# A second-level seven-product step for the fourth product of a gate-and-up block, with kept parts and right operands in DRAM

## The chip, the cores and the metric

One core of a Trainium2 chip runs the whole program. The metric is the device time of one execution in microseconds (us). The kernel before takes 1083.45 us (median of three runs, 1083.03 to 1083.62).

## The reference

The input `x` has 2 batches of 2048 rows of 512 numbers, all float32. First comes attention over channels (the scores are 512 by 512 for each batch) with a layer norm ahead of it and a residual, then a gated feed-forward block with its own layer norm and residual. The weights of the feed-forward block are given as indices into a table of 16 numbers:

```python
def _ghost_linear(x, idx, lut):
    w = lut[idx]
    return jnp.einsum('bsh,oh->bso', x, w)
gate = _ghost_linear(x, gate_idx, lut)     # idx: (1376, 512)
up = _ghost_linear(x, up_idx, lut)         # idx: (1376, 512)
h = jax.nn.silu(gate) * up
return _ghost_linear(h, down_idx, lut)     # idx: (512, 1376)

x = x + _L0_attn_ref(_layernorm(x, axis=-1), Wq, Wk, Wv, Wo)
x = x + _L0_ffn_ref(_layernorm(x, axis=-1), lut, gate_idx, up_idx, down_idx)
```

The change is in the part that computes `gate` and `up`.

## The kernel before

**Stages.** By the profile's times: the Gram matrices and the small attention products come first, then (up to 286 us) the attention output `y`, then gate and up (286 to 806 us), then the down product (to the end). The order of the instructions on TensorE, ScalarE, VectorE and SyncE is the order in which the program's text makes them (a manual schedule); GpSimd's DMAs are in text order too.

**Units of gate and up.** The 1376 hidden channels are cut into 11 blocks `f` of 128 (the last has 96), the 4096 rows into 4 pairs `p` of two 512-row halves. A unit `(f, p)` is one 2-by-2 block product: the left operand has gate weights in its upper row (A11, A12) and up weights in its lower row (A21, A22); the right operand is the normalised input (`xs[p]`). The four blocks of the result are gate and up, each for two row halves. A unit does it by seven products in place of eight (Strassen's scheme in Winograd's form), with left sums S1 to S4 and right sums T1 to T4. Each product contracts 256 channels: two matmuls of 128x128 by 128x512 in float32, and each of those is two instructions in the profile.

**Steps of a unit**, as `Line.run` writes them: `a1` (A11·B11 into PSUM bank `a`, copied by ScalarE to `p1`), `c1` (S3·T3 into bank `c`, copied to `p7`), `extra1`, then `a4` of the unit before (S4·B22 onto its bank `a`, Silu by ScalarE), `a2` (S2·T2 onto `a`, copied to `u2`), `extra2`, `c2` (A22·T4 onto `c`, added to `u2` by VectorE), `end` of the unit before, `b` (A12·B21, then Silu of the gate half `h0`), `a3` (S1·T1 onto `a`, VectorE makes `c22` from it), `first` (`h0` times `u2`, stored to DRAM). Between the steps `between()` writes pieces of other VectorE work, chiefly the look-ups of weights (`pump`, `Job.ops`: 19 VectorE operations for each of 33 blocks of indices). Four of the products (`a1`, `a2`, `a3`, `a4`) are added up in bank `a`, and what stands there is copied out in between: a step that adds onto a bank can't begin before that copy is done.

```python
u.a2()
self.between()
u.extra2()
u.c2()
if last is not None:
    last.end()
self.between()
one, two = (u.a3, u.b) if final else (u.b, u.a3)
```

**Two levels for one product.** For the blocks `f` from 2 to 9 the product A12·B21 is itself done by seven products for eight over a group of four units: two blocks `f`, `f+1` and two row pairs `p`, `p+1`. The unit's `role` is its place in the group: 0 is (even f, even p), 1 is (even f, odd p), 2 is (odd f, even p), 3 is (odd f, odd p). Role 0 does two single matmuls in `b`, role 1 three (`extra1`, `extra2`, `b`), role 2 two (`extra1`, `b`), role 3 none. What roles 2 and 3 need of role 1 and 2 is kept in SBUF (`r6`, `r5`) and added onto `p1` by an accumulating DMA from GpSimd's queue (L938, L973).

**PSUM.** Eight banks: `a`, `b` and `c` with two buffers each, `x` and `y` with one.

**Look-ups.** `jobs` is the order of the blocks of indices. A job waits (its gate) until buffers are free. The indices are fetched by GpSimd's queue two jobs ahead and converted by ScalarE (`cast`).

Of the kernel before, what the change touches and what calls it, by code (L numbers as in the profile page):

```python
# [58 lines left out]
P = 128  # L60
# [6 lines left out]
def tile_attn_ffn(  # L67
# [228 lines left out]
    l2a, l2b = {}, {}  # L296
    whole = set()
# [3 lines left out]
    def gate_job(f):  # L301
        f0, rows = FT[f]
        n = KB * rows

        def load(queue, idx):
            queue.dma_start(idx, gate_idx[:, KB * f0 : KB * f0 + n])

        def dest():
            t = wgu.tile([P, KB, P], F32, tag="wg", name=f"wg_{f}", bufs=3)
            gw[f] = t.rearrange("p k r -> p (k r)")[:, :n]  # L310
            return gw[f]

        def after():
            gw[f] = gw[f].rearrange("p (k r) -> p k r", k=KB)
            whole.add(f)
            yield 0.1

        return Job(f"g{f}", P, n, load, dest, after, lambda: f < 3 + passed[0])

    def up_job(f):  # L320
        f0, rows = FT[f]
        n = KB * rows
        up = []

        def load(queue, idx):
            queue.dma_start(idx, up_idx[:, KB * f0 : KB * f0 + n])

        def dest():
            t = wgu.tile([P, KB, P], F32, tag="wu", name=f"wu_{f}", bufs=2)
            up.append(t.rearrange("p k r -> p (k r)")[:, :n])  # L330
            return up[0]

        def after():
            g, u = gw[f], up[0].rearrange("p (k r) -> p k r", k=KB)
            t = wgu.tile([P, 3, 2, P], F32, tag="s", name=f"s_{f}", bufs=2)
            a11, a12, a21, a22 = g[:, 0:2, :], g[:, 2:4, :], u[:, 0:2, :], u[:, 2:4, :]
            s1, s2, s4 = (t[:, q, :, :rows] for q in range(3))
            for op, d, v, w in (
                (add, s1, a21, a22), (sub, s2, s1, a11), (sub, a21, a11, a21), (sub, s4, a12, s2)
            ):  # L340
                op(d, v, w)
                yield 0.42
            gu[f] = {"11": a11, "12": a12, "S3": a21, "22": a22, "S1": s1, "S2": s2, "S4": s4}
        return Job(f"u{f}", P, n, load, dest, after, lambda: f < 2 + ended[0])
# [10 lines left out]
    jobs += [down_job(i) for i in range(6)]  # L355
    for f in range(2, NFT - 1, 2):
        jobs += [gate_job(f), up_job(f), gate_job(f + 1), up_job(f + 1), down_job(5 + f // 2)]
# [19 lines left out]

    def pump(us):

        owed[0] = min(owed[0] + us, 2 * us + 1.0)  # L380
        while owed[0] > 0:
            cost = next(lookup, None)
            if cost is None:
                return
            owed[0] -= cost
# [474 lines left out]
    def psum(tag, name):  # L860
        return fps.tile([P, E], F32, tag=tag, name=name, bufs=1 if tag in "xy" else 2)

    def l2_sums(g):

        x11, x21 = xb[4 * g][:, 2, :], xb[4 * g][:, 3, :]
        x12, x22 = xb[4 * g + 2][:, 2, :], xb[4 * g + 2][:, 3, :]
        t = x2p.tile([P, 3, CH], F32, tag=f"l{g}", name=f"l2b_{g}")
        t1, t2, t4 = (t[:, q, :] for q in range(3))
        l2b[g] = {"11": x11, "21": x21, "22": x22, "T1": t1, "T2": t2, "T3": x12, "T4": t4}
        return [  # L870
            lambda: sub(t1, x12, x11), lambda: sub(t2, x22, t1),
            lambda: sub(x12, x22, x12), lambda: sub(t4, x21, t2),
        ]

    def l2_left(f):


        t = wgu.tile([P, 4, P], F32, tag="l", name=f"l_{f}", bufs=1)
        if f == NFT - 1:
            a12 = gu[f]["12"]  # L880
            both, minus = (t[:, q, : FT[f][1]] for q in range(2))
            gu[f]["both"], gu[f]["minus"] = both, minus
            return [
                lambda: add(both, a12[:, 0, :], a12[:, 1, :]),
                lambda: nc.vector.tensor_scalar_mul(minus, a12[:, 0, :], -1.0),
            ]
        a11, a12 = gw[f][:, 2, :], gw[f][:, 3, :]
        a21, a22 = gw[f + 1][:, 2, :], gw[f + 1][:, 3, :]
        s1, s2, s3, s4 = (t[:, q, :] for q in range(4))
        l2a[f // 2] = {"22": a22, "S1": s1, "S2": s2, "S3": s3, "S4": s4}  # L890
        return [
            lambda: add(s1, a21, a22), lambda: sub(s2, s1, a11),
            lambda: sub(s3, a11, a21), lambda: sub(s4, a12, s2),
        ]
# [8 lines left out]

    two = {}

    class GateUp:
# [8 lines left out]
        def pairs(self, a, b):  # L915
            return [(gu[self.f][a][:, kk, :], xs[self.p][b][:, kk, :]) for kk in range(2)]
# [11 lines left out]
        def a1(self):  # L928
            self.a = self.view("a")
            mm(self.a, self.pairs("11", "11"), True)  # L930
            if self.role in (None, 0):
                self.p1 = self.view("b")
            else:
                self.p1 = self.temp("p1")
            nc.scalar.copy(self.p1, self.a)
            if self.role in (2, 3):
                r = two["r6" if self.role == 2 else "r5", self.p // 2]
                nc.gpsimd.dma_start(self.p1, r, accum_op=ALU.add)  # L938

        def c1(self):  # L940
            self.c = self.view("c")
            mm(self.c, self.pairs("S3", "T3"), True)
            self.p7 = self.temp("p7")
            nc.scalar.copy(self.p7, self.c)  # L944

# [5 lines left out]
        def c2(self):  # L951
            mm(self.c, self.pairs("22", "T4"), False)
            add(self.u2, self.c, self.u2)

        def pair(self, a, b):
            return [(l2a[self.f // 2][a], l2b[self.p // 2][b])]

        def kept(self, tag):
            return x2p.tile([P, CH], F32, tag=f"{tag}{self.p // 2}", name=f"{tag}_{self.name}")

        def extra1(self):
            if self.role == 1:
                mm(two["x"], self.pair("S2", "T2"), False)
                two["r6", self.p // 2] = r6 = self.kept("r6")
                nc.scalar.copy(r6, two["x"])
            elif self.role == 2:
                two["y"] = self.view("y")
                mm(two["y"], self.pair("S3", "T3"), True)  # L970
                r7 = x2p.tile([P, CH], F32, tag="r7", name=f"r7_{self.name}")
                nc.scalar.copy(r7, two["y"])
                nc.gpsimd.dma_start(two["r5", self.p // 2], r7, accum_op=ALU.add)  # L973

        def extra2(self):
            if self.role == 1:
                mm(two["x"], self.pair("S1", "T1"), False)
                two["r5", self.p // 2] = r5 = self.kept("r5")
                nc.scalar.copy(r5, two["x"])

        def b(self):
            self.h0 = h0 = self.temp("h0", 2)
            g = self.p // 2
            if self.role is None:
                if self.f == NFT - 1 and self.p % 2:
                    x22, t3 = l2b[g]["22"], l2b[g]["T3"]
                    w = gu[self.f]
                    mm(self.p1, [(w["both"], x22), (w["minus"], t3)], False)
                else:
                    mm(self.p1, self.pairs("12", "21"), False)  # L990
            elif self.role == 0:
                two["x"] = self.view("x")
                mm(two["x"], [(gw[self.f][:, 2, :], l2b[g]["11"])], True)
                mm(self.p1, [(gw[self.f][:, 3, :], l2b[g]["21"])], False)
                nc.scalar.copy(h0, two["x"])
                add(h0, self.p1, h0)
            elif self.role == 1:
                mm(two["x"], self.pair("S4", "22"), False)
                add(h0, two["x"], self.p1)
            elif self.role == 2:  # L1000
                mm(two["y"], self.pair("22", "T4"), False)
                add(h0, two["y"], self.p1)
# [7 lines left out]
        def first(self):  # L1010
            nc.vector.tensor_tensor(self.h0, self.h0, self.u2, ALU.mult)
            self.store(self.h0, 2 * self.p)

        def a4(self):
# [3 lines left out]
            self.h1 = self.temp("h1", 2)  # L1018
# [6 lines left out]
    class Line:  # L1025
# [5 lines left out]
        def run(self, u, final=False):  # L1031
            u.a1()
            self.between()
            u.c1()
# [24 lines left out]

    sums_of = []  # L1060
    todo = []

    def between():
# [3 lines left out]
        elif sums_of and (sums_of[0] | 1) in whole:  # L1067
            for op in l2_left(sums_of.pop()):
                op()
        else:  # L1070
            pump(1.0)
# [81 lines left out]
    class Down:  # L1153
# [95 lines left out]
        extra1 = extra2 = first  # L1249
# [15 lines left out]
    for f, p in units:  # L1265
        while f not in gu or 1 < f < NFT - 1 and p and (f | 1) not in whole:
            next(lookup)
# [3 lines left out]
        elif sums_of:  # L1271
            for op in l2_left(sums_of.pop()):
                op()
        if f == NFT - 1 and p == 0:
# [9 lines left out]
            todo += by_two(l2_left(f) + down_sums(hps["dT"]))  # L1284
# [5 lines left out]
        line.run(GateUp(f, p), final=(f, p) == (NFT - 1, NPR - 1))  # L1290
# [5 lines left out]
        if f == 1 and p % 2:  # L1296
            todo += l2_sums(p // 2)
# [84 lines left out]
```

## Time and profile before

| | |
|---|---|
| time, median of three runs | 1083.45 us |
| time of the profiled execution | 1082.97 us |
| its span, first to last instruction | 1081.2 us |
| TensorE busy | 1075.6 us (99%), clock 1.000 |
| VectorE busy | 742.4 us (69%) |
| ScalarE busy | 340.1 us (31%) |
| GpSimd busy | 57.7 us (5%) |
| VectorE busy from 450 to 500 us | 40.98 us of 50 |
| DMA share from 450 to 500 us | 0.27 |

Matmuls are pipelined: a group of four instructions is shown as 1.88 us long, but the next group starts 1.72 us after it. "Idle before" is the time for which an engine had nothing to do before an instruction, with what released it. PEld is the load of the weights ahead of a matmul.

### The profile page before, as it was taken

What the parts mean: (1) busy time and instruction counts of PE and PEld (TensorE: products, weight loads), DVE (VectorE), ACT (ScalarE), POOL (GpSimd) and SP (SyncE); (2) the same over time, 40 slices, a digit from 0 to 9 for tenths busy, and PEclk for the clock granted to TensorE, in tenths of its full rate; (3) what the DMA queues carried; (4) which work ended last, traced back from release to release, by engine and by line L of the source; (5) the groups of instructions that cost most, each with busy time, mean ns of one, the idle gap of its engine ahead of it and who ended that gap; (6) DMA issues with size and microseconds to landing.
All of it is one profiled execution on the core that took longest, in us unless ns stands there. A gap on an engine that the chain in (4) does not pass through costs nothing.

```text
span 1081.2 us, 10377 instructions
## 1 busy us (share of the span) xinstructions
PE 1075.6 (99%) x3442; PEld 644.9 (60%) x3442; DVE 742.4 (69%) x1610; ACT 340.1 (31%) x631; POOL 57.7 (5%) x94
## 2 busy tenths in 40 slices
PE   9999999999999999999999999999999999999998
PEld 5668886444444444444444444444348888888887
DVE  7888777899888778888787887876643334433341
ACT  4652522555632233323332332333221111111110
POOL 0000000012110000100110020010000000000000
PEclk9999999999999999999999999999999999999999
DMA  8750314597661111331231142123425545345421
GB/s 342 232 166 17 81 40 97 139 231 205 169 163 49 49 50 67 98 84 53 78 97 64 54 109 76 54 74 80 149 58 168 179 155 163 93 141 183 154 68 39
DMA packets 91061, 123.44 MB, mean 114 GB/s; under 512 B 14576, under 2 KB 50672, under 8 KB 90112
## 3 DMA queue, kind: packets, MB, share of 16 engines
q1 hardware_dynamic: 62496, 83.39, 24.4%
q0 software_dynamic: 8448, 22.62, 9.4%
q10 hardware_dynamic: 20064, 16.78, 4.9%
q8 instruction: 27, 0.44, 0.2%
q14 instruction: 26, 0.21, 0.1%
HBM read 68.76 MB, written 47.71 MB: 108 GB/s over the span
## 4 chain that ended last, share of the span: by engine, by line
PE 93%; DVE 4%; ACT 2%; issue 1%; ACTq 0%; DMA 0%; DVEq 0%
PE a_g L899 28%; PE a_d L899 14%; PE c_g L899 14%; PE y L754 8%; PE c_d L899 7%; PE gp L438 4%; PE b_d L899 4%; PE b_g L899 3%; PE x_g L899 3%; PE ea_t L591 1%; PE ea_p L591 1%; PE ea_m L591 1%; PE y_g L899 1%; PE ea_s L591 1%; PE ec_p L591 1%; PE ec_m L591 1%
## 5 line engine op out<-in xcount | busy, mean ns | idle before, releaser
L754 PE MATMUL y<-m,nT 128*128 128x512 f32 x256 | 110.4, 592 | 0.0
L135 DVE TENSOR_TENSOR u<-c_g,u 128x512 f32<-128x512 f32 (+1 forms) x44 | 30.4, 691 | 102.0 <-PE c_g L899 102.0
L754 PEld LDWEIGHTS y<-m,nT 128*128 128x128 f32 x256 | 48.5, 190 | 60.7 <-issue 57.3
L899 PE MATMUL a_g<-xb,wg 128*128 128x512 f32 (+1 forms) x176 | 82.7, 592 | 0.0
L899 PE MATMUL c_g<-xb,wu 128*128 128x512 f32 (+1 forms) x176 | 82.7, 592 | 0.0
L899 PE MATMUL a_g<-xb,s 128*128 128x512 f32 (+1 forms) x176 | 82.7, 592 | 0.0
L899 PE MATMUL a_g<-xT_a,s 128*128 128x512 f32 (+1 forms) x176 | 82.7, 592 | 0.0
L438 PE MATMUL gp<-xn_a 128*128 128x128 f32 (+3 forms) x256 | 70.1, 434 | 0.4 <-ACT xn_a L231 0.3
L899 PE MATMUL a_g<-xT_sq,s 128*128 128x512 f32 (+1 forms) x132 | 62.0, 592 | 0.0
L438 PEld LDWEIGHTS gp<-xn_a 128*128 128x128 f32 x256 | 43.9, 190 | 27.7 <-issue 15.1
L899 PEld LDWEIGHTS a_g<-xb,s 128*128 128x128 f32 (+1 forms) x176 | 33.0, 188 | 42.6 <-issue 38.2
L899 PEld LDWEIGHTS a_g<-xT_a,s 128*128 128x128 f32 (+1 forms) x176 | 33.0, 188 | 42.5 <-issue 42.5
L899 PEld LDWEIGHTS c_g<-xb,wu 128*128 128x128 f32 (+1 forms) x176 | 33.0, 188 | 42.5 <-issue 42.5
L899 PEld LDWEIGHTS a_g<-xb,wg 128*128 128x128 f32 (+1 forms) x176 | 33.0, 188 | 42.5 <-issue 42.3
L289 DVE COPY_PREDICATED wd<-b_wd,wd 128x512 f32<-128x512 int16 (+1 forms) x77 | 56.4, 733 | 1.6
L899 PE MATMUL a_d<-dT,hs_a 128*128 128x256 f32 x224 | 56.2, 378 | 0.0
L135 DVE TENSOR_TENSOR r<-r,a_d 128x256 f32<-128x256 f32 x32 | 13.5, 421 | 53.4 <-PE a_d L899 53.4
L899 PEld LDWEIGHTS a_d<-dT,hs_a 128*128 128x128 f32 x224 | 42.4, 189 | 6.0
L277 DVE TENSOR_SCALAR wd<-idx_wd,lut_x,lut_sb 128x512 int32<-128x512 int32 (+1 forms) x88 | 44.5, 538 | 0.0
L899 PEld LDWEIGHTS a_g<-xT_sq,s 128*128 128x128 f32 (+1 forms) x132 | 24.8, 188 | 31.9 <-issue 31.3
L899 PE MATMUL c_g<-xT_a,wu 128*128 128x512 f32 (+1 forms) x88 | 41.5, 593 | 0.2 <-ACT p L944 0.2
L944 ACT COPY p<-c_g 128x512 f32<-128x512 f32 (+1 forms) x44 | 25.8, 585 | 48.2 <-PE c_g L899 43.5
(285 smaller groups left out, 1926.2 us busy)
## 6 DMA issues: line engine op xcount, KB each, us to landing
hd<-h SPq DMA_DIRECT2D x80, 256.0 KB, 2.0
h<-hd SPq DMA_DIRECT2D x40, 512.0 KB, 6.3
nl<-nd SPq DMA_DIRECT2D x32, 256.0 KB, 5.6
xnd<-xn_f ACTq DMA_DIRECT2D x16, 512.0 KB, 5.5
fl<-xnd POOLq DMA_DIRECT2D x32, 256.0 KB, 6.5
xn_back<-xnd SPq DMA_DIRECT2D x32, 256.0 KB, 3.5
out_dram<-r SPq DMA_DIRECT2D x31, 256.0 KB, 2.9
x<-in_x_dram SPq DMA_DIRECT2D x7, 1024.0 KB, 13.8
```

The costliest lines, as they stand in the source:

```text
L135: nc.vector.tensor_tensor(dest, a, b, ALU.add)
L277: vec.tensor_scalar(dest.bitcast(I32), idx, lut_x[:rows, k : k + 1], lut_i[:rows, at : at + 1], ALU.bitwise_and, ALU.bitwise_xor,)
L289: vec.copy_predicated(dest, masks[level - 1], t)
L438: nc.tensor.matmul(gp[b][i][:, i * P :], xn[:, i, j % 2, :], xn[:, i:, j % 2, :], start=c % CPB == 0 and j == 0, stop=c % CPB == CPB - 1 a ...
L591: nc.tensor.matmul(ps[:, m, :], self.a[a][:, k, m * P : (m + 1) * P], self.b[b][:, k, :], start=first and m == k == 0, stop=k == 1, skip_g ...
L754: nc.tensor.matmul(ys[k], nTs[k][:, i, :], m[:, i, :], start=(i == 0), stop=(i == KB - 1))
L899: nc.tensor.matmul(ps, lhsT, rhs, start=first and i == 0, stop=i == len(pairs) - 1, skip_group_check=not first,)
L944: nc.scalar.copy(self.p7, self.c)
```

## The change

The product A22·T4 (in `c2`) is now done over the same groups of four units by seven products for eight, as A12·B21 is. The bank `y` is gone and a bank `z` stands in its place: `x` serves A12·B21 in all roles, `z` serves A22·T4. Role 0 does two single matmuls in `c2` (one of them into `z`); role 1 three (a new step `extra0`, `extra1`, `c2`); role 2 two (`extra0`, `c2`); role 3 none. `c2` of role 3 issues nothing. The right operands' sums and the kept parts of both products go to DRAM and are loaded again or added from there: the kept parts are added by GpSimd's accumulating DMAs onto `p1` as before and, for the new product, onto a new copy `v` of bank `c`. `uw` keeps the looked-up weights of up; their sums (`of_both`) are put off, so that up's look-ups run one block ahead (three buffers of `wu` for two). `h0` and `h1` have one buffer for two. The order of the jobs and the rate of `pump` change.

```diff
-        return fps.tile([P, E], F32, tag=tag, name=name, bufs=1 if tag in "xy" else 2)
+        return fps.tile([P, E], F32, tag=tag, name=name, bufs=1 if tag in "xz" else 2)
...
+    class Second:
...
+            def made(tag, u, v):
+                r[tag] = x2p.tile([P, CH], F32, tag="rt", name=f"{tag}_{self.name}{g}", bufs=3)
+                sub(r[tag], u(), v())
+                far = self.far[g, tag] = dram.tile(
...
+                nc.sync.dma_start(far, r[tag])
...
+        def load(self, g, *tags):
+            for tag in tags:
+                t = x2p.tile([P, CH], F32, tag="tt", name=f"{tag}_{self.name}{g}_in", bufs=7)
+                nc.sync.dma_start(t, self.far[g, tag])
+                self.right[g][tag] = t
...
+        def part(self, u, tag, onto=False):
...
+            t = x2p.tile([P, CH], F32, tag="rt", name=f"{tag}_{self.name}_{u.name}", bufs=3)
+            nc.scalar.copy(t, self.ps)
+            if onto:
+                nc.gpsimd.dma_start(self.parts[g, tag], t, accum_op=ALU.add)
+                return
...
+            nc.sync.dma_start(to, t)
+
+        def add_part(self, u, dest):
+            tag = {2: "r6", 3: "r5"}.get(u.role)
+            if tag:
+                nc.gpsimd.dma_start(dest, self.parts[u.p // 2, tag], accum_op=ALU.add)
...
+    of_b = Second("b", "x", lambda f: in_two(gw[f][:, 2:4, :]), lambda p: in_two(xs[p]["21"]))
+    of_c = Second("c", "z", lambda f: in_two(uw[f][:, 2:4, :]), lambda p: in_two(xs[p]["T4"]))
...
+        def extra0(self):
+            if self.role == 1:
+                of_c.go_on(self, "S2", "T2")
+                of_c.part(self, "r6")
+            elif self.role == 2:
+                of_c.begin(self, "S3", "T3")
+                of_c.part(self, "r5", onto=True)
...
         def c1(self):
...
             nc.scalar.copy(self.p7, self.c)
+            if self.role in (2, 3):
+                self.v = self.temp("v")
+                nc.scalar.copy(self.v, self.c)
+                of_c.add_part(self, self.v)
...
         def c2(self):
-            mm(self.c, self.pairs("22", "T4"), False)
-            add(self.u2, self.c, self.u2)
...
+            if self.role is None:
+                mm(self.c, self.pairs("22", "T4"), False)
+                add(self.u2, self.c, self.u2)
+            elif self.role == 0:
+                of_c.begin(self, "11", "11")
+                mm(self.c, of_c.pair(self, "12", "21"), False)
+                add(self.u2, of_c.ps, self.u2)
+                add(self.u2, self.c, self.u2)
+            elif self.role == 1:
+                add(self.u2, self.c, self.u2)
+                of_c.go_on(self, "S4", "22")
+                add(self.u2, of_c.ps, self.u2)
+            elif self.role == 2:
+                of_c.go_on(self, "22", "T4")
+                add(self.u2, of_c.ps, self.u2)
+                add(self.u2, self.v, self.u2)
...
         def extra1(self):
             if self.role == 1:
...
+                of_c.go_on(self, "S1", "T1")
+                of_c.part(self, "r5")
+                of_b.go_on(self, "S2", "T2")
+                of_b.part(self, "r6")
             elif self.role == 2:
...
+                of_b.begin(self, "S3", "T3")
+                of_b.part(self, "r5", onto=True)
...
         def extra2(self):
             if self.role == 1:
...
+                of_b.go_on(self, "S1", "T1")
+                of_b.part(self, "r5")
...
         def first(self):
+            if self.role == 3:
+                add(self.u2, self.v, self.u2)
...
             u.a1()
             self.between()
+            u.extra0()
             u.c1()
...
+        u = GateUp(f, p)
+        pace[0] = {1: 1.2, 3: 0.8}.get(u.role, 1.07)
```

More of the change, by code (lines that the diff above doesn't have):

```diff
@@ L295, in tile_attn_ffn @@
     gw, gu = {}, {}
-    l2a, l2b = {}, {}
-    whole = set()
+    uw = {}
+    deferred = []
     passed = [0]
@@ L314, in after @@
             gw[f] = gw[f].rearrange("p (k r) -> p k r", k=KB)
-            whole.add(f)
             yield 0.1
@@ L328, in dest @@
         def dest():
-            t = wgu.tile([P, KB, P], F32, tag="wu", name=f"wu_{f}", bufs=2)
+            t = wgu.tile([P, KB, P], F32, tag="wu", name=f"wu_{f}", bufs=3)
             up.append(t.rearrange("p k r -> p (k r)")[:, :n])
@@ L333, in after, with of_both @@
         def after():
-            g, u = gw[f], up[0].rearrange("p (k r) -> p k r", k=KB)
+            uw[f] = up[0].rearrange("p (k r) -> p k r", k=KB)
+            deferred.append((lambda: f < 2 + ended[0], of_both()))
+            yield 0.1
+        def of_both():
+            g, u = gw[f], uw[f]
             t = wgu.tile([P, 3, 2, P], F32, tag="s", name=f"s_{f}", bufs=2)
@@ L343, in after @@
             gu[f] = {"11": a11, "12": a12, "S3": a21, "22": a22, "S1": s1, "S2": s2, "S4": s4}
-        return Job(f"u{f}", P, n, load, dest, after, lambda: f < 2 + ended[0])
+        return Job(f"u{f}", P, n, load, dest, after, lambda: f < 3 + ended[0])
     def down_job(i):
@@ L354, in tile_attn_ffn @@
     jobs = [job(f) for f in range(2) for job in (gate_job, up_job)]
-    jobs += [down_job(i) for i in range(6)]
+    jobs += [down_job(i) for i in range(4)]
     for f in range(2, NFT - 1, 2):
-        jobs += [gate_job(f), up_job(f), gate_job(f + 1), up_job(f + 1), down_job(5 + f // 2)]
+        jobs += [gate_job(f), up_job(f), gate_job(f + 1), up_job(f + 1)]
+        jobs += [down_job(i) for i in {2: (4,), 4: (5, 6), 6: (7,), 8: (8, 9)}[f]]
     jobs += [gate_job(NFT - 1), up_job(NFT - 1), down_job(NFT - 1)]
@@ L376, in tile_attn_ffn, with step @@
     owed = [0.0]
+    def step():
+        while deferred and deferred[0][0]():
+            cost = next(deferred[0][1], None)
+            if cost is not None:
+                return cost
+            deferred.pop(0)
+        return next(lookup, None)
     def pump(us):
@@ L381, in pump @@
         while owed[0] > 0:
-            cost = next(lookup, None)
+            cost = step()
             if cost is None:
@@ L860, in psum @@
     def psum(tag, name):
-        return fps.tile([P, E], F32, tag=tag, name=name, bufs=1 if tag in "xy" else 2)
[L863 to L882, printed above, removed]
+        return fps.tile([P, E], F32, tag=tag, name=name, bufs=1 if tag in "xz" else 2)
+    class Second:
+        def __init__(self, name, tag, weights, operand):
+            self.name, self.tag, self.weights, self.operand = name, tag, weights, operand
+            self.right, self.far, self.parts = {}, {}, {}
+        def sums(self, g):
+            (b11, b21), (b12, b22) = (self.operand(2 * g + h) for h in range(2))
+            r = self.right[g] = {"11": b11, "21": b21, "22": b22, "T3": b12}
+            def made(tag, u, v):
+                r[tag] = x2p.tile([P, CH], F32, tag="rt", name=f"{tag}_{self.name}{g}", bufs=3)
+                sub(r[tag], u(), v())
+                far = self.far[g, tag] = dram.tile(
+                    [P, CH], F32, tag=f"{self.name}{g}{tag}", name=f"far_{self.name}{g}{tag}"
+                )
+                nc.sync.dma_start(far, r[tag])
@@ L883, in l2_left @@
             return [
-                lambda: add(both, a12[:, 0, :], a12[:, 1, :]),
-                lambda: nc.vector.tensor_scalar_mul(minus, a12[:, 0, :], -1.0),
-            ]
[L887 to L894, printed above, removed]
+                lambda: made("T1", lambda: b12, lambda: b11),
@@ new lines, in sums, with sums_left @@
+                lambda: made("T2", lambda: b22, lambda: r["T1"]),
+                lambda: sub(b12, b22, b12),
+                lambda: made("T4", lambda: b21, lambda: r["T2"]),
+            ]
+        def load(self, g, *tags):
[3 more added lines that the diff above has]
+                self.right[g][tag] = t
+        def sums_left(self, f):
+            pool = wgu if self is of_b else x2p
+            t = pool.tile([P, 4, P], F32, tag=f"l{self.name}", name=f"l{self.name}_{f}", bufs=1)
+            (a11, a12), (a21, a22) = self.weights(f), self.weights(f + 1)
+            s1, s2, s3, s4 = (t[:, q, :] for q in range(4))
+            self.left = {"22": a22, "S1": s1, "S2": s2, "S3": s3, "S4": s4}
+            return [
+                lambda: add(s1, a21, a22), lambda: sub(s2, s1, a11),
+                lambda: sub(s3, a11, a21), lambda: sub(s4, a12, s2),
+            ]
@@ new lines, in pair, with begin, go_on @@
+        def pair(self, u, a, b):
+            if a in ("11", "12"):
+                left = self.weights(u.f)[a == "12"]
+            else:
+                left = self.left[a]
+            return [(left, self.right[u.p // 2][b])]
+        def begin(self, u, a, b):
+            self.ps = u.view(self.tag)
+            mm(self.ps, self.pair(u, a, b), True)
+        def go_on(self, u, a, b):
+            mm(self.ps, self.pair(u, a, b), False)
+        def part(self, u, tag, onto=False):
+            g = u.p // 2
+            t = x2p.tile([P, CH], F32, tag="rt", name=f"{tag}_{self.name}_{u.name}", bufs=3)
[3 more added lines that the diff above has]
+                return
+            to = self.parts[g, tag] = dram.tile(
+                [P, CH], F32, tag=f"{self.name}{g}{tag}", name=f"part_{tag}_{self.name}_{u.name}"
+            )
+            nc.sync.dma_start(to, t)
@@ new lines, in add_part, with in_two, there @@
+        def add_part(self, u, dest):
+            tag = {2: "r6", 3: "r5"}.get(u.role)
+            if tag:
+                nc.gpsimd.dma_start(dest, self.parts[u.p // 2, tag], accum_op=ALU.add)
+    def in_two(t):
+        return t[:, 0, :], t[:, 1, :]
+    of_b = Second("b", "x", lambda f: in_two(gw[f][:, 2:4, :]), lambda p: in_two(xs[p]["21"]))
+    of_c = Second("c", "z", lambda f: in_two(uw[f][:, 2:4, :]), lambda p: in_two(xs[p]["T4"]))
+    seconds = [of_b, of_c]
+    def there(f):
+        return f in gw and len(gw[f].shape) == 3 and f in uw
@@ new lines, in sums_left, with sums_last @@
+    def sums_left(f):
+        return [op for o in seconds for op in o.sums_left(f)]
+    def sums_last(f):
+        t, ops = wgu.tile([P, 4, P], F32, tag="lb", name=f"l_{f}", bufs=1), []
+        for i, a in enumerate(("12", "22")):
+            a1, a2 = in_two(gu[f][a])
+            both, minus = (t[:, 2 * i + q, : FT[f][1]] for q in range(2))
+            gu[f]["both" + a], gu[f]["minus" + a] = both, minus
+            ops += [
+                lambda v=(both, a1, a2): add(*v),
+                lambda v=(minus, a1, -1.0): nc.vector.tensor_scalar_mul(*v),
+            ]
+        return ops
@@ L896, in mm, with loads @@
+    def loads(f, p):
+        g = p // 2
+        if 1 < f < NFT - 1 and f % 2 == 0 and p % 2:
+            for tag in ("T2", "T1"):
+                for o in (of_c, of_b):
+                    o.load(g, tag)
+        elif 1 < f < NFT - 1 and f % 2 and p % 2 == 0:
+            for o in (of_c, of_b):
+                o.load(g, "T4")
     def mm(ps, pairs, first):
@@ L902, in mm @@
             )
-    two = {}
     class GateUp:
@@ L915, in pairs @@
         def pairs(self, a, b):
-            return [(gu[self.f][a][:, kk, :], xs[self.p][b][:, kk, :]) for kk in range(2)]
+            w, x = gu[self.f], xs[self.p][b]
+            if self.f == NFT - 1 and self.p % 2 and "both" + a in w and b in ("21", "T4"):
+                return [(w["both" + a], x[:, 1, :]), (w["minus" + a], x[:, 0, :])]
+            return [(w[a][:, kk, :], x[:, kk, :]) for kk in range(2)]
         def view(self, tag):
@@ L935, in a1 @@
             nc.scalar.copy(self.p1, self.a)
-            if self.role in (2, 3):
-                r = two["r6" if self.role == 2 else "r5", self.p // 2]
-                nc.gpsimd.dma_start(self.p1, r, accum_op=ALU.add)
+            of_b.add_part(self, self.p1)
+        def extra0(self):
[5 more added lines that the diff above has]
+                of_c.part(self, "r5", onto=True)
         def c1(self):
@@ L951, in c2 @@
         def c2(self):
-            mm(self.c, self.pairs("22", "T4"), False)
-            add(self.u2, self.c, self.u2)
[L955 to L959, printed above, removed]
+            if self.role is None:
[14 more added lines that the diff above has]
+                add(self.u2, self.v, self.u2)
@@ L963, in extra1 @@
         def extra1(self):
             if self.role == 1:
-                mm(two["x"], self.pair("S2", "T2"), False)
-                two["r6", self.p // 2] = r6 = self.kept("r6")
-                nc.scalar.copy(r6, two["x"])
+                of_c.go_on(self, "S1", "T1")
+                of_c.part(self, "r5")
+                of_b.go_on(self, "S2", "T2")
+                of_b.part(self, "r6")
             elif self.role == 2:
-                two["y"] = self.view("y")
-                mm(two["y"], self.pair("S3", "T3"), True)
@@ L971, in extra1 @@
-                r7 = x2p.tile([P, CH], F32, tag="r7", name=f"r7_{self.name}")
-                nc.scalar.copy(r7, two["y"])
-                nc.gpsimd.dma_start(two["r5", self.p // 2], r7, accum_op=ALU.add)
+                of_b.begin(self, "S3", "T3")
+                of_b.part(self, "r5", onto=True)
         def extra2(self):
             if self.role == 1:
-                mm(two["x"], self.pair("S1", "T1"), False)
-                two["r5", self.p // 2] = r5 = self.kept("r5")
-                nc.scalar.copy(r5, two["x"])
+                of_b.go_on(self, "S1", "T1")
@@ L981, in b @@
+                of_b.part(self, "r5")
         def b(self):
-            self.h0 = h0 = self.temp("h0", 2)
-            g = self.p // 2
+            self.h0 = h0 = self.temp("h0")
             if self.role is None:
[L985 to L990, printed above, removed]
+                mm(self.p1, self.pairs("12", "21"), False)
@@ L991, in b @@
             elif self.role == 0:
[L992 to L995, printed above, removed]
+                of_b.begin(self, "11", "11")
+                mm(self.p1, of_b.pair(self, "12", "21"), False)
+                nc.scalar.copy(h0, of_b.ps)
                 add(h0, self.p1, h0)
             elif self.role == 1:
-                mm(two["x"], self.pair("S4", "22"), False)
@@ L999, in b @@
-                add(h0, two["x"], self.p1)
+                of_b.go_on(self, "S4", "22")
+                add(h0, of_b.ps, self.p1)
             elif self.role == 2:
-                mm(two["y"], self.pair("22", "T4"), False)
-                add(h0, two["y"], self.p1)
+                of_b.go_on(self, "22", "T4")
+                add(h0, of_b.ps, self.p1)
             nc.scalar.activation(h0, self.p1 if self.role in (None, 3) else h0, AF.Silu)
@@ L1017, in a4 @@
                 ended[0] = self.f + 1
-            self.h1 = self.temp("h1", 2)
+            self.h1 = self.temp("h1")
             nc.scalar.activation(self.h1, self.a, AF.Silu)
@@ L1058, in flush @@
             self.last = None
+    pace = [1.0]
     sums_of = []
@@ L1066, in between @@
             pump(0.3)
-        elif sums_of and (sums_of[0] | 1) in whole:
-            for op in l2_left(sums_of.pop()):
+        elif sums_of and there(sums_of[0] | 1):
+            for op in sums_left(sums_of.pop()):
                 op()
         else:
-            pump(1.0)
+            pump(pace[0])
     def late(i, turned=(), pair=None):
@@ L1247, in first @@
             pass
-        extra1 = extra2 = first
+        extra0 = extra1 = extra2 = first
         def end(self):
@@ L1264, in tile_attn_ffn @@
     line = Line(between)
-    for f, p in units:
-        while f not in gu or 1 < f < NFT - 1 and p and (f | 1) not in whole:
-            next(lookup)
+    for (f, p), following in zip(units, units[1:] + [(NFT, 0)]):
+        while f not in gu or 1 < f < NFT - 1 and p and not there(f | 1):
+            step()
         assert p in xs
@@ L1271, in tile_attn_ffn @@
         elif sums_of:
-            for op in l2_left(sums_of.pop()):
+            for op in sums_left(sums_of.pop()):
                 op()
@@ L1283, in tile_attn_ffn @@
             h = Hidden(0)
-            todo += by_two(l2_left(f) + down_sums(hps["dT"]))
+            todo += by_two(sums_last(f) + down_sums(hps["dT"]))
         if f == NFT - 1 and p == 1:
@@ L1289, in tile_attn_ffn @@
             units = [Down(h, 0)]
-        line.run(GateUp(f, p), final=(f, p) == (NFT - 1, NPR - 1))
+        loads(*following)
+        u = GateUp(f, p)
+        pace[0] = {1: 1.2, 3: 0.8}.get(u.role, 1.07)
+        line.run(u, final=(f, p) == (NFT - 1, NPR - 1))
         if p == NPR - 1:
@@ L1296, in tile_attn_ffn @@
         if f == 1 and p % 2:
-            todo += l2_sums(p // 2)
+            todo += by_two([op for o in seconds for op in o.sums(p // 2)])
     for op in todo:
```

## The prediction

> **What bounds the kernel now.** I read the page first, then the waits of TensorE, then the order of time around single units. The page, with VectorE's row of the 40 slices of the span:
>
> ```profile
> PE 1075.6 (99%) x3442; PEld 644.9 (60%) x3442; DVE 742.4 (69%) x1610; ACT 340.1 (31%) x631; POOL 57.7 (5%) x94
> ...
> DVE  7888777899888778888787887876643334433341
> ```
>
> TensorE is the bound, busy for 99% at a clock of 1.000. VectorE is at eight tenths in gate and up (slices 10 to 28). The waits of TensorE over the whole span:
>
> ```profile
> PE idle L418 <- POOL ident masks.py:199: 1.4, 1, 1.4
> PE ea_s L591 <- ACT a L612: 0.3, 1, 0.3
> PE gp L438 <- ACT xn_a L231: 0.3, 1, 0.3
> PE c_g L899 <- ACT p L944: 0.2, 1, 0.2
> ```
>
> So gate and up has a single gap, and its length is its matmuls alone. This is a role 3 unit, (5,1), in order of time, TensorE and ScalarE only:
>
> ```profile
> 542.05 1.88 PE L899 MATMUL a_g<-xT_a,s 128*128 128x512 f32 x4
> ...
> 543.76 1.88 PE L899 MATMUL c_g<-xT_a,wu 128*128 128x512 f32 x4
> ...
> 543.97 0.59 ACT L949 COPY u<-a_g 128x512 f32<-128x512 f32 x1 [1.12 <-PE a_g L899]
> ...
> 545.48 1.88 PE L899 MATMUL a_g<-xT_a,s 128*128 128x512 f32 x4
> ```
>
> These are `a2`, `c2`, the copy of `a2`'s result to `u2`, and `a3`. Groups of four start 1.716 us apart, so one product of one 128-row block (two instructions) is 0.858 us. The copy starts 0.20 us after the next group's start and lasts 0.59: it ends 0.79 us into `c2`, and `a3`, which adds onto the same bank, comes 1.72 us after `a2`. `c2` hides the copy.
>
> The one gap shows what it costs when nothing hides a copy:
>
> ```profile
> 289.20 1.88 PE L899 MATMUL a_g<-xT_sq,s 128*128 128x512 f32 x4
> ...
> 290.70 0.56 ACT L944 COPY p<-c_g 128x512 f32<-128x512 f32 x1
> ...
> 291.31 1.98 PE L899 MATMUL c_g<-xT_a,wu 128*128 128x512 f32 x4 [0.23 <-ACT p L944]
> ...
> 293.13 0.59 PE L899 MATMUL b_g<-xb,wg 128*128 128x512 f32 x1
> ```
>
> The group should have started at 289.20 + 1.716 = 290.92. From the next group, 293.13 - 1.716, it started in effect at 291.41: 0.49 us lost, though the listed idle time is 0.23. The copy ended at 291.26, so TensorE is back 0.15 us after a copy's end.
>
> **What is removed.** The order of the changed kernel's instructions has 1719 matmuls for 1727. The eight that go are 128x512: one for each of 8 groups of four units. 8 x 0.858 = 6.87 us, all on the path, since TensorE has no gaps.
>
> **A new wait, role 3.** `c2` of role 3 issues nothing now, nor do `extra2` and `b`. In the changed order the matmuls of `a2` and of `a3` of these units follow each other directly, on the same bank, and `a3` waits for ScalarE's copy to `u2`. TensorE then stands for 0.20 + 0.59 + 0.15 = 0.94 us. Everything behind `a3` on TensorE's queue waits too, and nothing else fills the gap. There are 8 role 3 units: 8 x 0.94 = 7.5 us. If the restart costs nothing it is 0.79 each, 6.3 in all; if the price is what the delayed group was longer than its pace (1.98 - 1.72 = 0.26), 1.05 each, 8.4.
>
> **A second one, role 1.** In `b`, S4·22 goes onto bank `x` after the copy of S1·T1 from it (`r5`). Between them lay `c2` with 1.72 us; now there is one matmul of 0.858 us. The copy needs 0.94: 0.08 us short, 8 times, 0.7 us (none to 1.5 us by the same two ends). All other copies still have 1.72 us or more of matmuls behind them: `r6` of the new product has `c1` (1.72), `u2` of role 2 has two singles (1.72).
>
> Sum for TensorE: -6.87 + 7.5 + 0.7 = +1.3 us, with ends of -0.6 and +3.0.
>
> **VectorE.** It must not become late. Added for each group: three 128x512 adds (`u2` from `z` twice more, from `v`), at 0.68 us each, 16.3 us in all; 16 right sums of 0.68 in place of 8; 16 more small sums. It has room: its waits in 400 to 760 us are nearly all these,
>
> ```profile
> DVE u L135 <- PE c_g L899: 67.6, 31, 6.1
> ```
>
> that is 19% of 360 us, or about 2 us a unit. I summed the changed order unit by unit, with the distance between neighbouring operations in the trace (0.61 for an add, 0.72 for a predicated copy, 0.51 for a table operation, scaled by 0.95 so that the same sum gives the measured 3.2 to 4.1 us from the `u2` add to `c22` before). Middle units come to 10.6 to 12.3 us in roles 0 to 2, against 12.0 to 13.7 of TensorE, and 7.1 to 8.0 in role 3 against 8.6 + 0.9. The tightest place is `c22` of role 2, which `a4` of the next unit waits for 3.43 us after `a3`. `c22` would start 1.4 to 2.4 us after `a3` and take 0.7; before, it started up to 2.05 us after with no gap. Only units (3,0) and (7,2) come near, for perhaps 0.3 us together. Look-ups forced in a lump ahead of a unit do not show in these sums.
>
> **ScalarE, DMAs, GpSimd.** 40 more copies at 0.59 us lift ScalarE from 31%; role 1, the fullest, has 9 operations in 13.7 us. SyncE's queue gets 92 more DMAs. The right operands are loaded one unit ahead, behind the `hd` store of the unit before (which waits for VectorE, some 3 us into the unit); 256 KB stores and loads take 2 to 4 us here, of 12. GpSimd issues four accumulating DMAs in a role 2 unit for two, 0.9 us each. What is new is a wait of VectorE: `u2` plus `v` needs `c1`, two copies, a DMA with a DRAM source, all in about 6 us. In role 2 the copy to `v` ends about 1.4 us after `c1`, the issue follows 0.3 later, and VectorE wants `v` at 6.1 us: 4.4 us for a landing. Behind that add on VectorE stand `h1`, `h0`, then `c22`, for which `a4` waits, with 0.5 to 1 us more in typical units. The nearest rows:
>
> ```profile
> fl<-xnd POOLq DMA_DIRECT2D x32, 256.0 KB, 6.5
> ...
> p<-r POOLq DMA_DIRECT2D x16, 256.0 KB, 3.5
> ```
>
> The second is the same accumulation from SBUF (3.3 to 5.0 us in this stage); the first is this queue with a DRAM source, four in a row at a DMA share of 0.8, while the fetches of indices from DRAM on it land in 2.9 us. I take 3.6 us, since the stage's share was 0.27 and the three extra transfers of a unit leave it near 0.7 at most: no cost. The ends are none and 6.5 us.
>
> A page of the Trainium skill speaks against the change here ("DMA: Bandwidth & Descriptors", section "Latency and other measured facts"): access to HBM takes 0.2 us on average but 2 us at high load. By it, as an estimate, `v` would land after 3.8 us or after 5.6 us; the first costs nothing, the second about 8 x 0.6 = 5 us on top of my sum. No row here shows an accumulation from DRAM.
>
> **Forecast.** The profiled execution took 1082.97 us, 0.48 below the median. 1082.97 + 1.3 + 0.3 = 1084.6 profiled, or 1085.0 against the median of 1083.45. A measurement can tell about 0.2% (2.2 us) from no change, so the likeliest is "same", on the slow side: the eight matmuls are paid for by a wait that their removal opens. Chance 0.60, of which 0.46 within 0.2% and 0.14 above it (the upper ends). Its own range is 1082.9 to 1087.
>
> **Rival 1, the change does what it says and no more.** The copy to `u2` would have to be out of the way of `a3`. For it: TensorE had no gap in some 500 us before. Against it: that was `c2`'s cover, and the order has none left. Time 1083.45 - 6.87 = 1076.6. Chance 0.10.
>
> **Rival 2, `v` comes late.** Place: `u2` plus `v` in `c2` of role 2. Price: from a landing of about 5 us on, every us more delays `a4` of the next unit by as much, 8 times; it decides (slower by over 2.2 us in all) from about 5.1 us, since 1.6 us is used already. At 6.5 us it is 8 x 1.5 = 12 us: 1097. For it: `fl` at 6.5, and `p<-r` once at 5.0. Against: the median of 3.5 and the low DMA share. Chance 0.15.
>
> **Rival 3, VectorE becomes the bound.** If its operations take 5% longer than in the trace (more DMA traffic, more waits on stores with single buffers of `h0` and `h1`), the margin of `c22` goes in most role 2 and half of the role 1 units: about 0.4 us x 12 = 5 us, 1090. For it: over 90% busy in middle units. Against: 0.9 us of new slack in every role 3 unit. Chance 0.15; a fifth of it stays within 0.2%.
>
> Chances: faster 0.10; same 0.46 + 0.03 = 0.49; slower 0.14 + 0.15 + 0.12 = 0.41. The range 1081.5 to 1090 holds the main case and most of rival 3; it leaves out rival 1 and the larger part of rival 2.
>
> **What would show it.** In the profile after: a wait of TensorE on bank `a` released by the copy to `u2`, 8 times, listed at 0.6 to 0.9 us; the start of `a3` 2.66 us after that of `a2` in role 3; gaps of about 0.1 us ahead of S4·22 on `x`; 16 fewer instructions on TensorE. Rival 1 would show no such wait; rival 2 VectorE idle ahead of `u2` plus `v`, released by a DMA, and landings over 5 us; rival 3 TensorE waiting for `c22` on VectorE with no idle time of VectorE in these units.

## The result and the profile after

The changed kernel takes 1091.69 us (median of four runs, 1090.39 to 1092.09) against 1083.53 us before (a fourth run moved that median from 1083.45): ratio 1.0074, 95% interval 1.0057 to 1.0092. It is 8.2 us slower. The four runs lie 1.7 us apart, and the two longest are at a granted clock of 0.998 where the profiled one is at 0.999. The profiled execution took 1090.39 us, its span is 1088.6 us, 7.4 us more than before. The head of the page after, with VectorE's row of the slices:

```profile
PE 1072.0 (98%) x3426; PEld 640.0 (59%) x3426; DVE 768.7 (71%) x1660; ACT 360.4 (33%) x671; POOL 79.7 (7%) x118
...
DVE  7888777889885988898888888887543334433341
```

There are 16 instructions fewer on TensorE, as forecast, and it is less busy; the time is longer since it now stands. The waits of TensorE from 300 to 810 us, where before there were none:

```profile
PE a_g L998 <- ACT u L1059: 5.4, 8, 0.7
PE a_g L998 <- DVE c L136: 3.3, 4, 1.5
PE z_g L998 <- DVE lc L133: 1.2, 1, 1.2
```

Units (3,0) and (3,1) in order of time, without the look-ups and the weight loads; the columns are start, length, engine, line, operation:

```profile
443.30 0.69 DVE L136 TENSOR_TENSOR u<-z_g,u 128x512 f32<-128x512 f32 x1 [1.19 <-PE z_g L998]
...
445.05 0.69 DVE L136 TENSOR_TENSOR u<-v,u 128x512 f32<-128x512 f32 x1 [1.06 <-DMA v<-part_r_c]
...
449.05 0.69 DVE L136 TENSOR_TENSOR c<-a_g,p 128x512 f32<-128x512 f32 x1
...
449.79 1.98 PE L998 MATMUL a_g<-xb,s 128*128 128x512 f32 x4 [0.58 <-DVE c L136]
...
451.61 1.88 PE L998 MATMUL a_g<-xT_a,s 128*128 128x512 f32 x4
...
453.52 0.58 ACT L1059 COPY u<-a_g 128x512 f32<-128x512 f32 x1 [0.61 <-PE a_g L998]
...
454.16 1.98 PE L998 MATMUL a_g<-xT_a,s 128*128 128x512 f32 x4 [0.68 <-ACT u L1059]
```

The lower half is the forecast wait: `a2` starts at 451.61, the copy to `u2` ends at 454.10, `a3` starts at 454.16. The upper half is the wait for `c22`, forecast at 0.3 us and with no part of `v` in it: VectorE stands 1.06 us for `v`, has other work without a break from 445.05 to 449.05, so `c22` ends late, and `a4` waits for it.

From the starts of neighbouring groups, less their 0.429 us an instruction, TensorE loses in gate and up: 8 x 0.94 = 7.5 us ahead of `a3` in role 3; 8 x 0.084 = 0.7 us on bank `x` in role 1; 4.6 us ahead of `a4`, for `c22` of role 2, in five of eight units (0.2 to 1.75 us each); 1.4 us once in (2,1), for `lc`. That is 14.2 us. Less the 6.9 us of matmuls, and the one gap of 0.5 us before, which is gone, it makes +6.8; the stage grew by 6.95 (286.02 to 815.33 us against 285.77 to 808.13, each up to the first matmul of the down product).

### The profile page after: what moved, and what is told of

Same layout as the page of the kernel before. It is cut to its first block, busy times and chain, and to the rows that moved or that the text cites. A ratio compares the mean times of both kernels' runs of the same rounds, so it can differ in the third digit from the quotient of the medians.

```text
span 1088.6 us, 10783 instructions
## 1 busy us (share of the span) xinstructions
PE 1072.0 (98%) x3426; PEld 640.0 (59%) x3426; DVE 768.7 (71%) x1660; ACT 360.4 (33%) x671; POOL 79.7 (7%) x118
## 4 chain that ended last, share of the span: by engine, by line
PE 86%; DVE 4%; DMA 4%; issue 3%; ACT 2%; POOL 1%; ACTq 0%; SPq 0%; POOLq 0%; DVEq 0%
PE a_g L998 22%; PE a_d L998 14%; PE y L770 10%; PE c_g L998 8%; PE c_d L998 7%; PE gp L454 4%; PE b_d L998 4%; PE z_g L998 3%; PE x_g L998 3%; PE b_g L998 3%; DMA v<-part_r_c 2%; PE ea_t L607 1%; PE ea_p L607 1%; PE ea_m L607 1%; DMA hd<-h 1%
## 5 line engine op out<-in xcount | busy, mean ns | idle before, releaser
L136 DVE TENSOR_TENSOR u<-c_g,u 128x512 f32<-128x512 f32 (+1 forms) x28 | 19.3, 690 | 46.9 <-PE c_g L998 31.7
L1109 ACT ACTIVATE h<-h 128x512 f32<-128x512 f32 x24 | 15.1, 631 | 84.8 <-DVE h L136 84.8
L1059 ACT COPY u<-a_g 128x512 f32<-128x512 f32 (+1 forms) x44 | 25.7, 585 | 46.7 <-PE a_g L998 42.8
```

The lines of the kernel that those rows point to most:

```text
L136: nc.vector.tensor_tensor(dest, a, b, ALU.add)
L1059: nc.scalar.copy(self.u2, self.a)
L1109: nc.scalar.activation(h0, self.p1 if self.role in (None, 3) else h0, AF.Silu)
```

## The experiments

**The copy with nothing behind it, in the kernel before.** Only the order of `c2` and `a3` in role 3 changes:

```diff
-            u.c2()
+            swap = getattr(u, "role", None) == 3
+            if not swap:
+                u.c2()
...
             two()
+            if swap:
+                u.c2()
```

> The kernel before, with c2 of role 3 written after a3: the same matmuls, but a3 directly behind a2. Theory: 8 waits of 0.93 us each and nothing else, since c22 is there made ahead of c2 and a4 comes later than before: 1083.5 + 7.5 = 1091.0. Rival, the wait is only the listed idle time of about 0.67 us: 1088.9. Rival, the copy is hidden or takes place of other waits: 1083.5.

Measured: 1091.12 us, ratio 1.0068 (1.0051 to 1.0085), +7.6 us. Its only waits of TensorE in this stage are eight for the copy and the old one of 0.2:

```profile
PE a_g L899 <- ACT u L949: 5.4, 8, 0.7
```

The listed 5.4 us are 7.5 of lost time: the listed idle time is 0.68 each, the starts show 0.94.

**`a4` behind `a2` in role 3.**

```diff
+            behind = getattr(u, "role", None) == 3
-            if last is not None:
+            if last is not None and not behind:
                 last.a4()
                 self.between()
             u.a2()
             self.between()
+            if behind:
+                last.a4()
+                self.between()
             u.extra2()
```

> Change: in role 3 alone, a4 of the unit before is written after a2 and no longer ahead of it. Theory: of the 14.2 us that TensorE stands in gate and up, 7.5 are the copy to u2 between a2 and a3 of role 3, and 4.6 are a4 of role 3 waiting for c22 of role 2, which is late because v lands late. With a4 between a2 and a3 the copy has 1.72 us of cover, and c22 has 1.72 us more time than its longest lateness (1.65 us). Both go: 1091.7 - 12.1 = about 1079.6, range 1078 to 1081. Rival, VectorE itself is the bound: its lateness only moves to the next wait, the 7.5 us alone are won: about 1084. Rival, the copies are not what costs: no gain, about 1091.

Measured: 1083.51 us, ratio 1.0003 (0.9993 to 1.0013), 8.2 us less than the changed kernel and 4 short of what I expected. Both waits are gone. Beside bank `x`, two stand there, the new one for `p` and the old one for `lc`:

```profile
PE a_g L998 <- ACT p L1035: 3.1, 4, 1.3
PE z_g L998 <- DVE lc L133: 1.8, 1, 1.8
```

The first is `a2` of role 3 waiting for the copy of `a1` to `p1`. That copy stands behind Silu of role 2 on ScalarE, Silu waits for the add to `h0` on VectorE, and that add stands behind the wait for `v`. In order of time, from unit (3,0) into (3,1):

```profile
446.38 0.69 DVE L136 TENSOR_TENSOR u<-v,u 128x512 f32<-128x512 f32 x1 [1.90 <-DMA v<-part_r_c]
...
448.66 0.68 DVE L136 TENSOR_TENSOR h<-x_g,p 128x512 f32<-128x512 f32 x1
...
449.38 0.63 ACT L1109 ACTIVATE h<-h 128x512 f32<-128x512 f32 x1 [5.94 <-DVE h L136]
449.92 0.57 ACT L1035 COPY p<-a_g 128x512 f32<-128x512 f32 x1
...
450.54 1.98 PE L998 MATMUL a_g<-xT_a,s 128*128 128x512 f32 x4 [0.85 <-ACT p L1035]
```

By the starts the wait for `p` is 4.2 us in four units, `lc` is 2.1. The number was the one of the rival "VectorE is the bound"; the next runs say that it was not its load alone.

**`v` without its transfer.**

```diff
                 nc.scalar.copy(self.v, self.c)
-                of_c.add_part(self, self.v)
```

> The changed kernel without the accumulating DMAs onto v (the kept parts of the new product are left out of the sum). Theory: VectorE no longer stands ahead of u2 plus v (11.4 us in 12 waits), c22 of role 2 is in time, 4.6 us of TensorE's waits go: 1091.7 - 4.6 = 1087, with 8 waits of the copy to u2 left. Rival, VectorE's load makes c22 late and v only takes idle time: the waits for c22 stay at 3 us or more, 1090 to 1092.

Measured: 1086.91 us (ratio to before 1.0031, 1.0018 to 1.0044). No wait for `c22` is left; the eight for the copy and one for `lc` stay:

```profile
PE a_g L998 <- ACT u L1058: 5.4, 8, 0.7
PE z_g L998 <- DVE lc L133: 1.5, 1, 1.5
```

VectorE does the same work there, so its load alone doesn't make `c22` late; with the wait for `v` on top it is.

**The add of `v` in `first`**, behind `c22` on VectorE's queue, with nothing left out:

```diff
             elif self.role == 2:
                 of_c.go_on(self, "22", "T4")
                 add(self.u2, of_c.ps, self.u2)
-                add(self.u2, self.v, self.u2)
...
-            if self.role == 3:
+            if self.role in (2, 3):
                 add(self.u2, self.v, self.u2)
```

> The changed kernel with the add of v to u2 in role 2 moved from c2 to first, behind c22 on VectorE (as role 3 has it). Theory: h1, h0 and c22 no longer stand behind the wait for v, v has some 4 us more, the waits of TensorE for c22 (4.6 us) go and nothing comes in their place: 1091.7 - 4.6 = 1087.1, as without the transfers (1086.9). Rival, VectorE is short of time and the wait returns at the store of h0 or at the next u2: 1089 to 1092.

Measured: 1086.44 us (ratio to before 1.0028, 1.0017 to 1.0038), 5.2 us less than the changed kernel. The landing of `v` is as late as it was (5.4 us), and no wait for `c22` is left:

```profile
PE a_g L998 <- ACT u L1059: 5.4, 8, 0.7
PE z_g L998 <- DVE lc L133: 1.4, 1, 1.4
```

**Why `v` lands late**: four runs with other sources and other company on GpSimd's queue.

```diff
-                of_c.add_part(self, self.v)
+                nc.gpsimd.dma_start(self.v, self.p7, accum_op=ALU.add)
```

> The changed kernel with the accumulating DMA onto v taking its source from SBUF (p7, the other copy of the same bank, so other numbers are added) in place of DRAM; number, size and order of transfers stay. Theory A, the DRAM source makes v late: the landing falls from 5.5 us to the 3.5 us of the kernel before, waits for c22 go, 1087. Theory B, the queue makes it late (the accumulations of role 2 stand one behind the other, and more traffic): the landing stays at 5 us or more, 1090 to 1092.

```diff
             if onto:
-                nc.gpsimd.dma_start(self.parts[g, tag], t, accum_op=ALU.add)
                 return
```

> The changed kernel without the two accumulating DMAs of role 2 onto the kept parts in DRAM (half of r5 is left out), so that p1's and v's transfers are alone on GpSimd's queue. Theory B, the accumulations ahead of and behind v on the same queue hold it up: the landing of v falls from 5.5 us to 4 us or less in role 2, and the waits for c22 go. Theory A, the DRAM source does it: the landing stays at 5 us or more. With a source in SBUF it was 5.1 us.

The third has the second edit and no accumulation onto `p1` either:

> The changed kernel without the accumulations onto p1 and onto the kept parts in DRAM (both are left out of the sums), so that v's transfer is the only accumulation. Landing so far: 5.5 us in the changed kernel, 5.1 with a source in SBUF, 4.7 without the accumulations onto the parts. Theory B, the queue: 3.6 to 4.0 us. Theory A, the source in DRAM: 4.5 us or more.

The fourth has all three:

> The same, with v's transfer taking its source from SBUF (p7, so other numbers are added). Theory B: 3.4 to 3.6 us, as the kernel before has it (3.5), and 0.4 below v alone with its source in DRAM, the same difference as in the full queue. Theory A: 3.5 us, and a full 1 us or more below v alone from DRAM.

The times are 1088.31 us (ratio 1.0039, 1.0024 to 1.0054) for the first and, of one run each, 1087.13, 1088.97 and 1086.09 us for the others. The 1.8 us between the second and the third do not come from gate and up, which takes 525.8 and 525.6 us: in the third this stage begins at 288.3 us, in the second at 286.2, and in the first 30 us the granted clock is 0.94 in the third and 1.00 in the second. The DMA issues, with the median time to landing in the last column, are for `v` from the changed kernel, alone from DRAM, and alone from SBUF:

```profile
v<-part_r_c POOLq DMA_DIRECT2D x16, 256.0 KB, 5.5
```

```profile
v<-part_r_c POOLq DMA_DIRECT2D x16, 256.0 KB, 4.2
```

```profile
v<-p POOLq DMA_DIRECT2D x16, 256.0 KB, 3.4
```

| median landing of `v`, us | source DRAM | source SBUF |
|---|---|---|
| all accumulations | 5.5 | 5.1 |
| without those onto the parts | 4.7 | - |
| `v` alone | 4.2 | 3.4 |

Both theories hold a share: the source costs 0.4 to 0.8 us, the other accumulations 1.3 to 1.7.

These medians mix eight role 2 units with eight of role 3, and the two differ. By one profile each, from DRAM, with all accumulations, without those onto the parts, and alone, `v` landed after 5.53, 4.05 and 4.14 us in role 2, and after 5.64, 5.45 and 4.27 in role 3, which issues none onto the parts. So where the wait for `c22` arises, in role 2, all of the 1.4 us over the landing alone came with the two accumulations onto the parts, close to what theory B had (4 us or less without them), and none with the one onto `p1`; in role 3 nearly all came with `p1`'s.

Waits for `c22` were 4.6 us at a median of 5.5, 2.1 at 5.1 and none at 4.7 and 4.2. In the changed kernel the five role 2 units with a wait have landings of 5.51 to 6.34 us, the three without 4.75 to 5.15. The accumulations left out also take their traffic with them (the DMA share in 430 to 478 us is 0.63 in the changed kernel and 0.39 with `v` alone); whether the order on the queue or the shared engines delay `v` was not told apart.

**One buffer more on the way to DRAM.**

```diff
-                r[tag] = x2p.tile([P, CH], F32, tag="rt", name=f"{tag}_{self.name}{g}", bufs=3)
+                r[tag] = x2p.tile([P, CH], F32, tag="rt", name=f"{tag}_{self.name}{g}", bufs=4)
...
-                t = x2p.tile([P, CH], F32, tag="tt", name=f"{tag}_{self.name}{g}_in", bufs=7)
+                t = x2p.tile([P, CH], F32, tag="tt", name=f"{tag}_{self.name}{g}_in", bufs=6)
...
```

> The changed kernel with four buffers for the sums and parts on their way to DRAM (rt) in place of three, and six in place of seven for the operands that come back (tt), since SBUF has no room for more. Theory: the single wait of TensorE in unit (2,1) for the last left sums (1.4 us) goes, since the right sums of VectorE no longer stand for 2.9 us until a store has freed a buffer; all else stays: 1091.7 - 1.4 = 1090.3. Rival, VectorE has too much to do in (2,0) (a forced lump of sums), and the buffer only takes idle time: the wait stays at 1 us or more.

Measured: 1091.55 us (ratio 1.0077, 1.0063 to 1.0091): no gain. In the changed kernel the cause of the wait for `lc` was this, in order of time in unit (2,0) and after:

```profile
388.69 0.69 DVE L133 TENSOR_TENSOR T_c<-xT_x,xT_sq 128x512 f32<-128x512 f32 x1 [2.88 <-DMA far_b1T<-T_b]
...
395.50 1.13 PE L998 MATMUL z_g<-T_c_in,lc 128*128 128x512 f32 x2 [1.17 <-DVE lc L133]
```

VectorE stood for a store that should free a buffer; with the fourth buffer the same stand (2.92 us) came one sum later, and `lc` behind it was as late. The store lands after 4.4 us (median of three), behind four loads of right operands on SyncE's queue, against 2.0 to 2.5 for the other sums.

**The edits together.** First `a4` behind `a2` and `v` in `first` alone:

> Only a4 behind a2 in role 3 and the add of v in first. Theory: 12.1 us of the 14.2 go, and the waits of bank x (0.7 us) and of lc (1.2 to 2 us) stay: 1091.7 - 12.1 = 1079.6 by the median of the changed kernel, 1078.2 by the version with four edits (1077.5) and the 0.7 us of bank x. Rival, the moved extra2 is what counts: 1083.

Measured: 1079.15 us, ratio 0.9959 (0.9947 to 0.9972). TensorE's losses by the starts are 1.7 us for `lc` and 8 x 0.084 on bank `x`, 2.4 in all. Next, with the four rt buffers and with `extra2` written ahead of `a2`:

```diff
+            u.extra2()
             u.a2()
             self.between()
...
-            u.extra2()
             u.c2()
```

> The changed kernel with four edits: a4 behind a2 in role 3; the add of v in first; extra2 ahead of a2 in role 1, which gives the copy from bank x 2.6 us of cover; rt with four buffers and tt with six. Theory: all 14.2 us of TensorE's new waits are accounted for by these four, so the eight matmuls taken out are left: 1083.5 - 6.9 = 1076.7, range 1076 to 1078.5. In the version with a4 behind a2 alone the wait came back as ScalarE's copy to p1 standing behind Silu, which stood behind v; with v in first that is gone too. Rival, VectorE is the bound: 1080 to 1084.

Measured: 1077.54 us, ratio 0.9949 (0.9935 to 0.9962); only the wait for `lc` is left (1.3 us by the starts). Last, three rt buffers again, and the left sums ahead of the right sums on VectorE:

```diff
-        if todo:
-            todo.pop(0)()
-            pump(0.3)
-        elif sums_of and there(sums_of[0] | 1):
+        if sums_of and there(sums_of[0] | 1):
             for op in sums_left(sums_of.pop()):
                 op()
+        elif todo:
+            todo.pop(0)()
+            pump(0.3)
```

> The changed kernel with a4 behind a2 in role 3, the add of v in first, extra2 ahead of a2 in role 1, three rt buffers again, and in between() the left sums of both products (lb, lc) ahead of the right sums that still wait to be made. Theory: the last wait, 1.2 us in unit (2,1) for lc, was the order on VectorE: lc stood behind a right sum that waits 2.9 us for a store to DRAM to free its buffer. With lc ahead TensorE has no gap in gate and up: 1083.5 - 6.9 = 1076.6, and 1.2 us below the version with four edits (1077.5): 1076.3 to 1076.7. Rival, the wait moves to the right operands T2 and T1, which come later: 1077.5.

Measured: 1076.25 us (1076.11 to 1076.45), ratio 0.9933 (0.9919 to 0.9946), 7.3 us below the kernel before. All waits of TensorE over the whole span of this version:

```profile
PE idle L434 <- POOL ident masks.py:199: 1.4, 1, 1.4
PE ea_s L607 <- ACT a L628: 0.3, 1, 0.3
PE gp L454 <- ACT xn_a L232: 0.3, 1, 0.3
PE gp L454 <- DVE xn_a L177: 0.2, 1, 0.2
```

None is in gate and up, and the stage is 7.2 us shorter than before: the eight matmuls and the old gap, within 0.15 us.

## Why the prediction was wrong

**What was removed: right.** 16 instructions went, 6.87 us.

**The wait of role 3: right in place and size.** Forecast 8 x 0.94 = 7.5 us, measured the same. The undoing in the kernel before gave +7.6 us for this alone. The profile's own figure would have misled: it lists 0.68 us for each.

**The wait of role 1: right**, 0.7 us.

**The landing of `v`: this term failed.** The sum took 3.6 us from the row of the kernel before and wrote "no cost", since the DMA share would stay near 0.7 at most. The share did stay below that (0.54 from 400 to 760 us), and the landing was 5.5 us all the same, 4.75 to 6.34 in role 2: the share did not tell it. The wait for it cost 4.6 us by the starts and 5.2 by the time that moving the add won. The place, the path (`u2` plus `v`, then `c22`, then `a4`) and the point of about 5 us were those of rival 2, which I gave 0.15; its price at 5.5 us, 8 x 0.5 = 4 us, is near the 4.6. The row was the same kind of transfer in other company: alone and from SBUF it does take 3.4. I had counted that a role 2 unit issues four accumulations where it issued two, and drew the conclusion for GpSimd's time and for the DMA share, not for the landing; the two onto the parts made 1.4 us there. Of the estimate from the Trainium skill ("DMA: Bandwidth & Descriptors", section "Latency and other measured facts"; 3.8 or 5.6 us for a source in HBM): alone, the source in DRAM added 0.8, between the page's 0.2 and 2. The 5.5 of the changed kernel is near 5.6, but of its 2.1 us over 3.4 the other accumulations make 1.3 to 1.7.

**VectorE's sums: right on load, wrong on a stand.** Without `v`'s transfer nothing waits for `c22`, so rival 3, VectorE's load alone, falls. But the unit sums held only work; in (2,0) VectorE also stood 2.9 us for a store to free a buffer, and `lc` came 1.4 us late. "Look-ups forced in a lump do not show" was true and beside the point.

**Together** the forecast was +1.6 us. With 4.3 more from `v` and 1.4 from `lc` that makes +7.3, near the 7.4 of the profiled span. In part this is luck: the old gap, which the forecast kept, went (0.5 less), and the stages on both sides of gate and up took 0.5 more, whose cause stays open. The median is 0.7 us further off than the profiled run, and the changed kernel's runs lie 1.7 us apart where those of the last version lie 0.3 apart. What scatters was not settled.

## What to carry to other kernels

When a step is emptied, look at what it stood between: a copy out of a bank that the next step adds onto needs 0.94 us of other matmuls here, and an order that puts any other bank's group there gives them for nothing. A transfer's landing is not a constant of its kind: take it with as many others under way as it will have, and put the add that waits for it behind everything that others wait for. When the wait moved instead of going (as with `a4` behind `a2`), following it back over two queues, ScalarE's and VectorE's, led to the same transfer.

## What the runs showed of the hardware

An accumulating DMA of 256 KB from GpSimd's queue lands after 3.4 us from SBUF and 4.2 from DRAM with no other accumulation in the stage. From DRAM with all of them it takes 5.5: in role 2 leaving out the two accumulations onto DRAM around it took 1.5 us off, in role 3 leaving out the one onto `p1` as well took 1.2 off. Accumulations onto DRAM land after medians of 5.5 and 6.2 us in the changed kernel. TensorE loses 0.94 us where the profile lists 0.68 of idle time: 0.1 is the longer first group (1.98 for 1.88 us), and 0.16 lies in how the end of the group before is drawn, since a group of 1.88 us is followed after 1.72 when nothing waits.
